# Folding the score maxima by DMA before they are turned, and turning the rows of both norms beside them

## The chip, the cores and the metric

The kernel runs on one core of a Trainium2 chip. A core has five engines that each take their own instructions in the written order and wait for one another by semaphores: PE (TensorE, matrix products and turns, written to PSUM), DVE (VectorE), ACT (ScalarE), POOL (GpSimd) and SP (SyncE, which here only issues DMAs). The metric is the device time of one execution in microseconds (us), the median over runs of the same kernel. A lower time is better.

## The reference, cut to what matters

One adaptive-norm transformer block on 8 sequences of 1024 tokens with 256 features: a norm with modulation, attention with 16 heads of 64 over 1024 keys, a gated residual, a second norm, and a mixture of 8 experts in which each expert takes its 512 best tokens. All of it is float32.

```python
h = _layernorm(x) * (1 + ca) + sa
q, k, v = ...                                  # einsum('bpv,havn->bhapn', h, w_qkv)
scores = einsum('bhqn,bhkn->bhqk', q, k) / sqrt(64)
attn = softmax(scores, axis=-1)                # exp(scores - max over keys), by its sum
x = x + ga * (einsum('bhqk,bhkn->bhqn', attn, v) ... @ w_o)
h = _layernorm(x) * (1 + cb) + sb
x = x + gb * ffn(h)                            # router, top 512 tokens of each of 8 experts, two layers
```

The change lies in the maximum over keys of the softmax and in the turning of the rows of both norms.

## The kernel before

The attention stage is a software pipeline. A **unit** `u` is one pair of heads of one sequence and half of its queries (512): 8 sequences x 8 pairs x 2 halves are 128 units (`NSU`). The 1024 keys of a unit are 8 blocks of 128 (`c`), and a **group** `g` is two of those blocks, so that a unit has four groups; `gm` is the group within the unit. The loop at L648 goes through the groups and writes each engine's instructions in the order in which the engine takes them: everything stands in a manual schedule.

For a block of keys, `scores_mm` (L306) makes two products, one for each head `j`, with keys on the partitions and queries along the free dimension, in one of two PSUM buffers with the tag "s". `scores_out` (L319) copies them to SBUF on ScalarE (L322) and folds them into a running maximum `top` of 128 x (2 x 512) on VectorE (L327). After the last block, `top` holds for every query 128 candidates, one per partition.

`max_turn` (L329) turns `top` on PE against an identity as eight blocks of 128 x 128 into a third use of the "s" buffers, so that the candidates of a query lie along the free dimension; `split_max` (L338) reduces them on VectorE over 128 x 1024 elements to 128 x 8 negated maxima and splits each into three bfloat16 parts (L342 to L350). `max_rows` (L352) turns the parts back to rows on PE, ScalarE copies the rows (L361), and `max_spread` (L363) adds the three parts by a product with ones, so that `less` has the negated maximum in every partition. `subtract` (L371), `exp_of` (L374), `values_mm` (L377) and POOL's `add_up` (L395) follow with a delay: subtractions of unit `u` start five groups after its first scores, values six.

In a group the order is: steps booked under "load" (DMAs), the spread, one or two delayed subtractions, the scores of two blocks with copies and maxima, the steps "m1" (projections `qk_task` and `v_task`, one in each group but the first; `max_rows` in the first), "post", the exponentials, two value products, in the last group `max_turn` and `split_max`, then "pool" and "m2". The work of other stages is booked into groups by `at(g, where, f, ...)`. Two of those stages turn rows of a norm: `ln_out` (L243, first norm, 32 calls) and `out_turn` (L522, second norm, 32 calls of which 28 lie in the pipeline). Both make a turn of 128 x 128 as two matmuls of 64 columns against the identity. `free_slot` (L597) gives these steps, and the output projection `out_proj` (L488), one slot each in a last group of a unit, behind the turn of the maxima. The denominators go through DRAM: `den_out`, `den_load`, `den_inv`, `den_spread`, `den_mul` (L408 to L469).

All DMAs of this stage are issued from SyncE, in the order of the program. After the pipeline come the tail of the last sequence, the search for each expert's tokens and the experts.

Of the kernel before, what the change touches and what calls it, by code (L numbers as in the profile page):

```python
# [28 lines left out]
F32 = mybir.dt.float32  # L29
BF16 = mybir.dt.bfloat16  # L30
# [12 lines left out]
def adaln_block(  # L43
# [171 lines left out]
    def at(g, where, f, *args):  # L215
        steps.setdefault((g, where), []).append((f, args))
# [26 lines left out]
    def ln_out(b, t):  # L243
        if t == 0:
            hTs[b] = work.tile([P, KC, S], F32, tag="hT", name=f"hT{b}")
        xt = ln_x.pop((b, t))[0]
        pt = ps_m.tile([P, KC, 2 * P], F32, tag="mm", name=f"ptx{b}_{t}")
        for k in range(KC):
            for i in range(2):
                for m in range(2):  # L250
                    c0 = k * P + m * N
                    nc.tensor.matmul(
                        pt[m * N : (m + 1) * N, k, i * P : (i + 1) * P],
                        xt[:, i, c0 : c0 + N], ident, start=True, stop=True,
                    )
        for k in range(KC):
            nc.vector.tensor_scalar(
                hTs[b][:, k, 2 * t * P : (2 * t + 2) * P], pt[:, k, :],
                modT[:, KC + k, b : b + 1], modT[:, k, b : b + 1],
                op0=ALU.mult, op1=ALU.add,  # L260
            )

    def ln_task(b, t, g):
        at(g - 4, "load", ln_load, b, t)
        at(g - 2, "post", ln_stats, b, t)
        at(g - 1, "pool", ln_norm, b, t)
        at(g, "m2", ln_out, b, t)


    def qk_task(b, p, i):  # L270
# [48 lines left out]
    def scores_out(u, c, ps):  # L319
# [6 lines left out]
            tops[u] = work.tile([P, 2, QB], F32, tag="top", name=f"top{u}", bufs=1)  # L326
        nc.vector.tensor_tensor(tops[u], probs[u, 0] if c == 1 else tops[u], ps, ALU.max)  # L327

    def max_turn(u):  # L329
        top = tops.pop(u)  # L330
        turned[u] = ps_s.tile([P, 8, P], F32, tag="s", name=f"tt{u}")
        for j in range(2):
            for t in range(4):
                nc.tensor.transpose(  # L334
                    turned[u][:, 4 * j + t, :], top[:, j, t * P : (t + 1) * P], ident
                )

    def split_max(u):  # L338

        tt = turned.pop(u)  # L340
        nm = tt[:, :2, :8]
        nc.vector.tensor_reduce(nm[:, 0, :], tt, AX.X, ALU.max, negate=True)  # L342
        part = [
            parts_of[u % 2][:, :, :, i].rearrange("p t j -> p j t") for i in range(3)
        ]
        whole, rest = (nm[:, i, :].rearrange("p (j t) -> p j t", j=2) for i in range(2))
        nc.vector.tensor_copy(part[0], whole)
        nc.vector.tensor_sub(rest, whole, part[0])
        nc.vector.tensor_copy(part[1], rest)
        nc.vector.tensor_sub(part[2], rest, part[1])  # L350

    def max_rows(u):  # L352
        pn = ps_m.tile([P, QB], BF16, tag="mm", name=f"pn{u}")
        for t in range(4):
            for j in range(2):
                nc.tensor.transpose(
                    pn[j * N : (j + 1) * N, t * P : (t + 1) * P],
                    parts_of[u % 2][:, t, j, :], ident_b,
                )
        rows_of[u] = work.tile([P, QB], BF16, tag="nr", name=f"nr{u}")  # L360
        nc.scalar.copy(rows_of[u], pn)  # L361

    def max_spread(u):  # L363

        less[u] = ps_b.tile([P, 2, QB], F32, tag="less", name=f"less{u}")
        rows = rows_of.pop(u)
        for j in range(2):
            r = slice(j * N, (j + 1) * N)
            nc.tensor.matmul(less[u][:, j, :], three[r, :], rows[r, :], start=True, stop=True)  # L369

    def subtract(u, c):  # L371
        nc.vector.tensor_tensor(probs[u, c], probs[u, c], less[u], ALU.add)  # L372
# [127 lines left out]
    def out_add(b, t, po):  # L500
        n = f"{b}_{t}"
        x1 = o_x[b, t]
        tmp = small.tile([P, D], F32, tag="at", name=f"at{n}", bufs=2)
        nc.vector.tensor_mul(tmp, po, mods[b][:, 0, :])
        nc.vector.tensor_add(x1[:, 0, :], x1[:, 0, :], tmp)
        nc.sync.dma_start(out[b, t * P : (t + 1) * P, :], x1[:, 0, :])
        o_h[b, t] = stats_of(small, x1, 1, f"b{n}")

    def out_norm(b, t):
        n = f"{b}_{t}"  # L510
        mv = o_h[b, t]
        rs = rstd_of(small, mv, 1, f"b{n}")
        x1 = o_x.pop((b, t))[:, 0, :]
        row = small.tile([P, ROW], F32, tag="row", name=f"row{n}", bufs=6)
        h2 = row[:, :D]
        eng = nc.vector if b == B - 1 else nc.gpsimd
        eng.tensor_scalar(h2, x1, mv[:, 0, 0:1], rs, op0=ALU.subtract, op1=ALU.mult)
        nc.gpsimd.tensor_mul(h2, h2, mods[b][:, 2, :])
        nc.gpsimd.tensor_add(h2, h2, mods[b][:, 1, :])
        o_h[b, t] = row  # L520

    def out_turn(pool, b, t, tag="mm"):  # L522

        n = f"{b}_{t}"
        pt = pool.tile([P, 2, KC, P], F32, tag=tag, name=f"pth{n}")
        for i in range(2):
            h2 = o_h[b, t + i]
            for k in range(KC):
                for m in range(2):
                    c0 = k * P + m * N  # L530
                    nc.tensor.matmul(
                        pt[m * N : (m + 1) * N, i, k, :], h2[:, c0 : c0 + N], ident,
                        start=True, stop=True,
                    )
        h2T = small.tile([P, 2, KC, P], F32, tag="h2T", name=f"h2T{n}", bufs=1)
        nc.scalar.copy(h2T, pt)
        o_x[b, t] = h2T
# [54 lines left out]
        )  # L592


    taken = set()

    def free_slot(g, behind=False):  # L597
        while g in taken or g % 4 == 0 or behind != (g % 4 == 3):
            g += 1
        taken.add(g)  # L600
        return g

    for t in range(NT // 2):
        ln_task(0, t, -23 + 3 * t)
        ln_task(1, t, free_slot(39 + 4 * t, True))
    for b in range(B):
        for p in range(NP):
            P0 = 8 * (b * NP + p)
            for i, g in enumerate((-7, -6, -5, -2)):
                at(P0 + g, "m1", qk_task, b, p, i)  # L610
            if p % 2 == 0:
                for t, g in enumerate((-9, -3, -1, 5)):
                    at(P0 + g, "m1", v_task, b, p // 2, t)
            if (b, p) == (B - 1, NP - 1):
                continue

            at(P0 + 17, "load", den_load, b, p)
            at(P0 + 18, "post", den_inv, b, p)
            at(P0 + 19, "load", den_spread, b, p)
            at(P0 + 20, "pool", den_mul, b, p)  # L620
        if b + 1 < B:
            if b + 2 < B:
                for t in range(NT // 2):
                    ln_task(b + 2, t, free_slot(64 * (b + 1) + 39 + 4 * t, True))
            for t in range(NT):
                g = free_slot(64 * (b + 1) + 19 + 4 * t, True)
                at(g - 2, "load", out_load, b, t)
                at(g, "m2", out_proj, ps_m, b, t)
                at(g + 1, "pool", out_norm, b, t)
                if t % 2:  # L630
                    g = free_slot(g + 2, True)
                    at(g, "m2", out_turn, ps_m, b, t - 1)
                    g = free_slot(g + 1)
                    at(g, "m2", out_route, ps_m, b, t - 1)
                    at(g + 1, "post", out_exp, b, t - 1)
                    at(g + 2, "post", out_score, b, t - 1)
                    at(g + 3, "pool", out_store, b, t - 1)
    for u in range(NSU):
        at(4 * u + 4, "m1", max_rows, u)
        if u < NSU - 1:  # L640
            at(4 * u + 12, "m2", den_out, u)
    for b in range(B):
        at(64 * b + 30, "load", gates, b)
    for t in range(NT):
# [2 lines left out]
    with tc.manual_schedule():  # L647
        g = -28  # L648
        while g < 4 * NSU + LAG or steps:
            u, gm = divmod(g, 4)  # L650
            run(g, "load")
            if gm == 1 and 0 < u <= NSU:
                max_spread(u - 1)
            u1, gm1 = divmod(g - LAG + 1, 4)
            late = [(u1, 2 * gm1 + i) for i in range(2) if 0 <= u1 < NSU]

            for uc in late[: 1 if gm == 3 else 2]:
                subtract(*uc)
            if 0 <= u < NSU:
                for c in (2 * gm, 2 * gm + 1):  # L660
                    scores_out(u, c, scores_mm(u, c))
            if gm == 3 and late:
                subtract(*late[1])
            run(g, "m1")
            run(g, "post")
            for uc in late:
                exp_of(*uc)
            u1, gm1 = divmod(g - LAG, 4)
            if 0 <= u1 < NSU:
# [7 lines left out]
                    values_out(u1)  # L677
                if u1 < NSU - 1:
                    add_up(u1, gm1)
            if gm == 3 and 0 <= u < NSU:  # L680
                max_turn(u)
                split_max(u)
            run(g, "pool")
            run(g, "m2")
            g += 1
# [342 lines left out]
```

## Time and profile before

| | us |
|---|---|
| median of 3 runs | 3648.16 (3646.65 to 3648.54) |
| profiled execution, its own time | 3645.84 |
| its span, first to last instruction | 3644.1 |
| PE busy | 3467.5 (95%) |
| DVE busy | 2902.9 (80%) |
| ACT busy | 2431.7 (67%) |
| POOL busy | 2668.6 (73%) |
| turn of the maxima, L334 on PE | 139.9 in 1024 instructions |
| reduction of the turned maxima, L342 on DVE | 157.4 in 128 |
| turns of the norms, L252 and L531 on PE | 39.0 and 39.6 in 512 instructions each |
| eviction of the first norm's turn, L257 on DVE | 31.7 in 64 |

Busy time is a union of the intervals in which an engine works; matmuls of one kind overlap, so that busy time over the count is less than the mean duration. A line such as `L334 PE MATMUL tt<-ident,top` names the line of the kernel, the engine, the operation, the tile written and those read. In a timeline the first column is the start in us from the span's start, the second the time that the merged instructions take; in brackets stands how long the engine was idle before them and who released it. In a list of waits, the numbers are the total in us, the count and the longest. DMA-issuing instructions on SyncE are short and don't contain the transfer.

### The profile page before, as it was taken

What the parts mean: (1) busy time and instruction counts of PE and PEld (TensorE: products, weight loads), DVE (VectorE), ACT (ScalarE), POOL (GpSimd) and SP (SyncE); (2) the same over time, 40 slices, a digit from 0 to 9 for tenths busy, and PEclk for the clock granted to TensorE, in tenths of its full rate; (3) what the DMA queues carried; (4) which work ended last, traced back from release to release, by engine and by line L of the source; (5) the groups of instructions that cost most, each with busy time, mean ns of one, the idle gap of its engine ahead of it and who ended that gap; (6) DMA issues with size and microseconds to landing.
All of it is one profiled execution on the core that took longest, in us unless ns stands there. A gap on an engine that the chain in (4) does not pass through costs nothing. (4 is left out here: it accounts for less than half of the span.)

```text
span 3644.1 us, 54310 instructions
## 1 busy us (share of the span) xinstructions
PE 3467.5 (95%) x20670; PEld 1461.3 (40%) x20670; DVE 2902.9 (80%) x3647; ACT 2431.7 (67%) x2978; POOL 2668.6 (73%) x1545
## 2 busy tenths in 40 slices
PE   5999999999999999999999999999999999982898
PEld 2333334334343444344343343344434334442565
DVE  3888888888888888888888888888888888857442
ACT  1777777777777777777777777777777777740111
POOL 1678777887788778888788888887888787851232
PEclk8999999999999999999999999999999999995999
DMA  3010002111120112011210113111211112133332
GB/s 76 7 39 27 24 31 58 49 38 45 45 62 30 52 48 66 29 45 45 62 52 29 51 50 62 30 50 46 62 38 43 46 48 59 51 85 122 93 99 41
DMA packets 189045, 185.40 MB, mean 51 GB/s; under 512 B 48856, under 2 KB 167144, under 8 KB 188656
## 3 DMA queue, kind: packets, MB, share of 16 engines
q1 hardware_dynamic: 159856, 156.62, 15.1%
q0 software_dynamic: 7168, 12.72, 1.7%
q10 hardware_dynamic: 21760, 12.59, 1.3%
q8 instruction: 163, 2.67, 0.3%
q14 instruction: 98, 0.80, 0.1%
HBM read 127.06 MB, written 63.21 MB: 52 GB/s over the span
## 5 line engine op out<-in xcount | busy, mean ns | idle before, releaser
L403 POOL TENSOR_TENSOR acc<-acc,p 128x1024 f32<-128x1024 f32 x762 | 1806.5, 2371 | 360.0 <-ACT p L375 327.0
L322 ACT COPY p<-s 128x1024 f32<-128x1024 f32 x1024 | 996.4, 1018 | 421.7 <-PE s L313 415.0
L372 DVE TENSOR_TENSOR p<-p,less 128x1024 f32<-128x1024 f32 x1024 | 1206.5, 1209 | 32.6 <-PE less L369 30.0
L327 DVE TENSOR_TENSOR top<-top,s 128x1024 f32<-128x1024 f32 x768 | 936.6, 1220 | 260.3 <-ACT p L322 219.3
L375 ACT ACTIVATE p<-p 128x1024 f32<-128x1024 f32 x1024 | 1041.8, 1057 | 74.7 <-DVE p L372 74.4
L313 PE MATMUL s<-qk,qk 64*128 64x512 f32 x4096 | 1025.8, 613 | 35.2 <-DVE parts L350 32.1
L384 PE MATMUL av<-p,v 128*64 128x512 f32 x4096 | 967.1, 593 | 1.8 <-ACT oT L393 1.8
L313 PEld LDWEIGHTS s<-qk,qk 64*128 64x128 f32 x4096 | 358.9, 187 | 527.4 <-issue 237.8
L278 PE MATMUL pq<-hT,wq 128*64 128x512 f32 x2048 | 495.9, 605 | 2.7 <-ACT qk L285 1.4
L384 PEld LDWEIGHTS av<-p,v 128*64 128x64 f32 x4096 | 280.6, 137 | 461.4 <-issue 366.9
L400 POOL TENSOR_TENSOR acc<-p,p 128x1024 f32<-128x1024 f32 x127 | 301.6, 2375 | 176.2 <-ACT p L375 176.2
L278 PEld LDWEIGHTS pq<-hT,wq 128*64 128x64 f32 x2048 | 124.2, 136 | 342.7 <-issue 211.4
L295 PE MATMUL pv<-wq,hT 128*64 128x256 f32 x2048 | 250.7, 387 | 2.6 <-ACT qk L283 1.4
L953 ACT ACTIVATE h<-ph,b_sb 128x512 f32<-128x512 f32 x64 | 44.0, 687 | 276.1 <-PE ph L949 276.1
L342 DVE TENSOR_REDUCE tt<-tt 128x8 f32<-128x1024 f32 x128 | 157.4, 1229 | 67.6 <-PE tt L334 67.5
L494 PE MATMUL po<-wo,ot 128*64 128x256 f32 x1792 | 205.7, 382 | 0.0
L295 PEld LDWEIGHTS pv<-wq,hT 128*64 128x64 f32 x2048 | 136.5, 137 | 155.7 <-issue 66.5
L327 DVE TENSOR_TENSOR top<-p,s 128x1024 f32<-128x1024 f32 x128 | 155.7, 1217 | 32.3 <-ACT p L322 32.3
L300 ACT COPY v<-pv 128x512 f32<-128x512 f32 x128 | 75.0, 586 | 148.4 <-PE pv L295 148.4
L334 PEld LDWEIGHTS tt<-ident,top 128*128 128x128 f32 x1024 | 109.6, 140 | 107.2 <-DVE top L327 107.2
L465 POOL TENSOR_TENSOR oT<-oT,rb 128x1024 f32<-128x1024 f32 x63 | 150.0, 2381 | 3.0 <-issue 3.0
L494 PEld LDWEIGHTS po<-wo,ot 128*64 128x64 f32 x1792 | 123.5, 137 | 66.2 <-issue 9.4
(161 smaller groups left out, 2442.8 us busy)
## 6 DMA issues: line engine op xcount, KB each, us to landing
rb<-rden_d SPq DMA_DIRECT2D x128, 256.0 KB
oT_d<-oT SPq DMA_DIRECT2D x62, 512.0 KB
ot<-oT_d SPq DMA_DIRECT2D x56, 512.0 KB
rows_d<-row SPq DMA_DIRECT2D x64, 132.0 KB
lnx<-in_L_attn_inputs_dram SPq DMA_DIRECT2D x32, 256.0 KB
rows_d<-gb_d SPq DMA_DIRECT2D x8, 1024.0 KB
w<-in_L_ffn_w_dram ACTq DMA_DIRECT2D x8, 1024.0 KB
w<-in_L_ffn_w_dram SPq DMA_DIRECT2D x8, 1024.0 KB
```

What stands on the lines that cost most here:

```text
L278: nc.tensor.matmul(pq[m * N : (m + 1) * N, :], wq[:, k, a, 2 * p + m, :], hTs[b][:, k, sl], start=(k == 0), stop=(k == KC - 1),)
L295: nc.tensor.matmul(pv[m * N : (m + 1) * N, i, :], hTs[b][:, k, t0 : t0 + N], wq[:, k, 2, 4 * g : 4 * g + 4, :], start=(k == 0), stop=(k == ...
L313: nc.tensor.matmul(ps[:, j, :], kt[r, c * P : (c + 1) * P], qt[r, h * QB : (h + 1) * QB], start=True, stop=True,)
L322: nc.scalar.copy(probs[u, c], ps)
L327: nc.vector.tensor_tensor(tops[u], probs[u, 0] if c == 1 else tops[u], ps, ALU.max)
L342: nc.vector.tensor_reduce(nm[:, 0, :], tt, AX.X, ALU.max, negate=True)
L372: nc.vector.tensor_tensor(probs[u, c], probs[u, c], less[u], ALU.add)
L375: nc.scalar.activation(probs[u, c], probs[u, c], AF.Exp)
L384: nc.tensor.matmul(avs[u][j * N : (j + 1) * N, :], v[:, c, hh * N : (hh + 1) * N], pT[:, j, :], start=(c == 0), stop=(c == NT - 1),)
L400: nc.gpsimd.tensor_tensor(sums[u], pts[0], pts[1], ALU.add)
L403: nc.gpsimd.tensor_tensor(sums[u], sums[u], pt, ALU.add)
L494: nc.tensor.matmul(po[m * N : (m + 1) * N, :], ot[:, p, m * N : (m + 1) * N], wo[:, p, :], start=(p == 0), stop=(p == NP - 1),)
```

## The change

`max_fold` is new: after the last maximum of a unit, four DMAs from SyncE copy the 64-partition halves of `top` into two tiles of 128 x 512 floats, so that partitions 0 to 63 hold head 0 and partitions 64 to 127 hold head 1, each with half of the candidates. `max_halves` takes the larger of the two on VectorE, in the first group of the next unit, between its two subtractions. `max_turn` then has four blocks instead of eight, written to PSUM behind that group's two scores, and `split_max` reduces 128 x 512 elements. Both stand in the first group of the next unit, behind "m1". A new kind of step, "turn", follows them at once, and the rows of both norms are turned there by four transposes of 128 x 128 for a call instead of eight matmuls of 64 columns. The first norm's eviction goes to ScalarE. `max_rows` moves from "m1" to "m2" of that group, the spread moves behind the scores of the second group, and the split of the subtractions ahead of and behind the scores changes with it. The first norm of the next sequence is booked earlier, the output projection goes to the third group of a unit, the denominator's steps move by one group, and three tiles (`nr`, `at`, `row`) get fewer buffers.

```diff
@@ -247,24 +247,20 @@
         pt = ps_m.tile([P, KC, 2 * P], F32, tag="mm", name=f"ptx{b}_{t}")
         for k in range(KC):
             for i in range(2):
-                for m in range(2):
-                    c0 = k * P + m * N
-                    nc.tensor.matmul(
-                        pt[m * N : (m + 1) * N, k, i * P : (i + 1) * P],
-                        xt[:, i, c0 : c0 + N], ident, start=True, stop=True,
-                    )
+                nc.tensor.transpose(
+                    pt[:, k, i * P : (i + 1) * P], xt[:, i, k * P : (k + 1) * P], ident
+                )
         for k in range(KC):
-            nc.vector.tensor_scalar(
-                hTs[b][:, k, 2 * t * P : (2 * t + 2) * P], pt[:, k, :],
-                modT[:, KC + k, b : b + 1], modT[:, k, b : b + 1],
-                op0=ALU.mult, op1=ALU.add,
+            nc.scalar.activation(
+                hTs[b][:, k, 2 * t * P : (2 * t + 2) * P], pt[:, k, :], AF.Identity,
+                bias=modT[:, k, b : b + 1], scale=modT[:, KC + k, b : b + 1],
             )
 
     def ln_task(b, t, g):
         at(g - 4, "load", ln_load, b, t)
         at(g - 2, "post", ln_stats, b, t)
         at(g - 1, "pool", ln_norm, b, t)
-        at(g, "m2", ln_out, b, t)
+        at(g, "turn", ln_out, b, t)
 
 
     def qk_task(b, p, i):
@@ -326,24 +322,38 @@
             tops[u] = work.tile([P, 2, QB], F32, tag="top", name=f"top{u}", bufs=1)
         nc.vector.tensor_tensor(tops[u], probs[u, 0] if c == 1 else tops[u], ps, ALU.max)
 
+    def max_fold(u):
+
+        top = tops[u]
+        tops[u] = [work.tile([P, QB], F32, tag=f"half{i}", name=f"half{i}_{u}", bufs=1) for i in range(2)]
+        for i in range(2):
+            for j in range(2):
+                src = (i + j) % 2
+                nc.sync.dma_start(
+                    tops[u][i][j * N : (j + 1) * N, :], top[src * N : (src + 1) * N, j, :]
+                )
+
+    def max_halves(u):
+        a, b = tops[u]
+        nc.vector.tensor_tensor(a, a, b, ALU.max)
+
     def max_turn(u):
-        top = tops.pop(u)
-        turned[u] = ps_s.tile([P, 8, P], F32, tag="s", name=f"tt{u}")
-        for j in range(2):
-            for t in range(4):
-                nc.tensor.transpose(
-                    turned[u][:, 4 * j + t, :], top[:, j, t * P : (t + 1) * P], ident
-                )
+        top = tops.pop(u)[0]
+        turned[u] = ps_s.tile([P, 2, QB], F32, tag="s", name=f"tt{u}")
+        for t in range(4):
+            sl = slice(t * P, (t + 1) * P)
+            nc.tensor.transpose(turned[u][:, 0, sl], top[:, sl], ident)
 
     def split_max(u):
 
         tt = turned.pop(u)
-        nm = tt[:, :2, :8]
-        nc.vector.tensor_reduce(nm[:, 0, :], tt, AX.X, ALU.max, negate=True)
-        part = [
-            parts_of[u % 2][:, :, :, i].rearrange("p t j -> p j t") for i in range(3)
-        ]
-        whole, rest = (nm[:, i, :].rearrange("p (j t) -> p j t", j=2) for i in range(2))
+        nm = tt[:, 1, :16].rearrange("p (i t j) -> p i t j", i=2, j=2)
+        part = [parts_of[u % 2][:, :, :, i] for i in range(3)]
+        whole, rest = nm[:, 0], nm[:, 1]
+        nc.vector.tensor_reduce(
+            whole, tt[:, 0, :].rearrange("p (t j k) -> p t j k", t=4, j=2), AX.X, ALU.max,
+            negate=True,
+        )
         nc.vector.tensor_copy(part[0], whole)
         nc.vector.tensor_sub(rest, whole, part[0])
         nc.vector.tensor_copy(part[1], rest)
@@ -357,7 +367,7 @@
                     pn[j * N : (j + 1) * N, t * P : (t + 1) * P],
                     parts_of[u % 2][:, t, j, :], ident_b,
                 )
-        rows_of[u] = work.tile([P, QB], BF16, tag="nr", name=f"nr{u}")
+        rows_of[u] = work.tile([P, QB], BF16, tag="nr", name=f"nr{u}", bufs=1)
         nc.scalar.copy(rows_of[u], pn)
 
     def max_spread(u):
@@ -500,7 +510,7 @@
     def out_add(b, t, po):
         n = f"{b}_{t}"
         x1 = o_x[b, t]
-        tmp = small.tile([P, D], F32, tag="at", name=f"at{n}", bufs=2)
+        tmp = small.tile([P, D], F32, tag="at", name=f"at{n}", bufs=1)
         nc.vector.tensor_mul(tmp, po, mods[b][:, 0, :])
         nc.vector.tensor_add(x1[:, 0, :], x1[:, 0, :], tmp)
         nc.sync.dma_start(out[b, t * P : (t + 1) * P, :], x1[:, 0, :])
@@ -511,7 +521,7 @@
         mv = o_h[b, t]
         rs = rstd_of(small, mv, 1, f"b{n}")
         x1 = o_x.pop((b, t))[:, 0, :]
-        row = small.tile([P, ROW], F32, tag="row", name=f"row{n}", bufs=6)
+        row = small.tile([P, ROW], F32, tag="row", name=f"row{n}", bufs=4)
         h2 = row[:, :D]
         eng = nc.vector if b == B - 1 else nc.gpsimd
         eng.tensor_scalar(h2, x1, mv[:, 0, 0:1], rs, op0=ALU.subtract, op1=ALU.mult)
@@ -526,12 +536,7 @@
         for i in range(2):
             h2 = o_h[b, t + i]
             for k in range(KC):
-                for m in range(2):
-                    c0 = k * P + m * N
-                    nc.tensor.matmul(
-                        pt[m * N : (m + 1) * N, i, k, :], h2[:, c0 : c0 + N], ident,
-                        start=True, stop=True,
-                    )
+                nc.tensor.transpose(pt[:, i, k, :], h2[:, k * P : (k + 1) * P], ident)
         h2T = small.tile([P, 2, KC, P], F32, tag="h2T", name=f"h2T{n}", bufs=1)
         nc.scalar.copy(h2T, pt)
         o_x[b, t] = h2T
@@ -592,17 +597,9 @@
         )
 
 
-    taken = set()
-
-    def free_slot(g, behind=False):
-        while g in taken or g % 4 == 0 or behind != (g % 4 == 3):
-            g += 1
-        taken.add(g)
-        return g
 
     for t in range(NT // 2):
         ln_task(0, t, -23 + 3 * t)
-        ln_task(1, t, free_slot(39 + 4 * t, True))
     for b in range(B):
         for p in range(NP):
             P0 = 8 * (b * NP + p)
@@ -614,31 +611,28 @@
             if (b, p) == (B - 1, NP - 1):
                 continue
 
-            at(P0 + 17, "load", den_load, b, p)
-            at(P0 + 18, "post", den_inv, b, p)
-            at(P0 + 19, "load", den_spread, b, p)
-            at(P0 + 20, "pool", den_mul, b, p)
+            at(P0 + 18, "load", den_load, b, p)
+            at(P0 + 19, "post", den_inv, b, p)
+            at(P0 + 20, "load", den_spread, b, p)
+            at(P0 + 21, "pool", den_mul, b, p)
         if b + 1 < B:
-            if b + 2 < B:
-                for t in range(NT // 2):
-                    ln_task(b + 2, t, free_slot(64 * (b + 1) + 39 + 4 * t, True))
+            for t in range(NT // 2):
+                ln_task(b + 1, t, 64 * b + 4 + 4 * t)
             for t in range(NT):
-                g = free_slot(64 * (b + 1) + 19 + 4 * t, True)
+                g = 64 * (b + 1) + 18 + 4 * t
                 at(g - 2, "load", out_load, b, t)
                 at(g, "m2", out_proj, ps_m, b, t)
                 at(g + 1, "pool", out_norm, b, t)
                 if t % 2:
-                    g = free_slot(g + 2, True)
-                    at(g, "m2", out_turn, ps_m, b, t - 1)
-                    g = free_slot(g + 1)
-                    at(g, "m2", out_route, ps_m, b, t - 1)
-                    at(g + 1, "post", out_exp, b, t - 1)
-                    at(g + 2, "post", out_score, b, t - 1)
-                    at(g + 3, "pool", out_store, b, t - 1)
+                    at(g + 6, "turn", out_turn, ps_m, b, t - 1)
+                    at(g + 9, "m2", out_route, ps_m, b, t - 1)
+                    at(g + 10, "post", out_exp, b, t - 1)
+                    at(g + 11, "post", out_score, b, t - 1)
+                    at(g + 12, "pool", out_store, b, t - 1)
     for u in range(NSU):
-        at(4 * u + 4, "m1", max_rows, u)
+        at(4 * u + 4, "m2", max_rows, u)
         if u < NSU - 1:
-            at(4 * u + 12, "m2", den_out, u)
+            at(4 * u + 13, "m2", den_out, u)
     for b in range(B):
         at(64 * b + 30, "load", gates, b)
     for t in range(NT):
@@ -649,19 +643,30 @@
         while g < 4 * NSU + LAG or steps:
             u, gm = divmod(g, 4)
             run(g, "load")
-            if gm == 1 and 0 < u <= NSU:
-                max_spread(u - 1)
             u1, gm1 = divmod(g - LAG + 1, 4)
             late = [(u1, 2 * gm1 + i) for i in range(2) if 0 <= u1 < NSU]
 
-            for uc in late[: 1 if gm == 3 else 2]:
+            early = {0: 2, 1: 0, 2: 2, 3: 1}[gm]
+            for i, uc in enumerate(late[:early]):
                 subtract(*uc)
+                if gm == 0 and i == 0 and 0 < u <= NSU:
+                    max_halves(u - 1)
             if 0 <= u < NSU:
                 for c in (2 * gm, 2 * gm + 1):
                     scores_out(u, c, scores_mm(u, c))
-            if gm == 3 and late:
-                subtract(*late[1])
+                if gm == 3:
+                    max_fold(u)
+            if gm == 1 and 0 < u <= NSU:
+                max_spread(u - 1)
+            for uc in late[early:]:
+                subtract(*uc)
             run(g, "m1")
+            if gm == 0 and 0 < u <= NSU:
+                if not late:
+                    max_halves(u - 1)
+                max_turn(u - 1)
+                split_max(u - 1)
+            run(g, "turn")
             run(g, "post")
             for uc in late:
                 exp_of(*uc)
@@ -677,9 +682,6 @@
                     values_out(u1)
                 if u1 < NSU - 1:
                     add_up(u1, gm1)
-            if gm == 3 and 0 <= u < NSU:
-                max_turn(u)
-                split_max(u)
             run(g, "pool")
             run(g, "m2")
             g += 1
```

## The prediction

> **What bounds the kernel now.** I read the stretches first. Three windows cut the attention stage into its start, a part and the rest; the columns are the stretch, then PE, PEld, DVE, ACT and POOL busy with instruction counts, granted clock, DMA share and GB/s.
>
> ```profile
> 85.00:600.00 515.00, 492.71 (x2740) 185.45 (x2740) 431.16 (x474) 393.10 (x471) 389.91 (x183) 1.00 0.10 28
> 600.00:1112.00 512.00, 509.57 (x3086) 204.40 (x3084) 437.70 (x530) 382.58 (x467) 420.94 (x239) 1.00 0.18 49
> 1112.00:3219.00 2107.00, 2094.05 (x12680) 840.21 (x12677) 1803.15 (x2153) 1577.29 (x1927) 1720.05 (x973) 1.00 0.17 47
> ```
>
> From 600 us on PE is busy 99.5% of the time at full clock; DVE is at 86%, ACT at 75%, POOL at 82%. The 128 units of the attention stage fill 85 to 3219 us, 24.7 us each, and PE sets that. So PE work removed is time won, and **any new wait on PE is time lost**, as PE takes its work in the written order.
>
> Next the waits, all engines, for what PE itself still waits on near the change:
>
> ```profile
> DVE top L327 <- ACT p L322: 251.6, 243, 22.4
> DVE tt L342 <- PE tt L334: 67.5, 99, 1.2
> PE s L313 <- DVE parts L350: 32.1, 71, 1.3
> ```
>
> PE loses 32.1 us to the split maxima (71 waits, because the turned maxima hold a scores buffer). Then the order of time, around the end of one unit:
>
> ```profile
> 1499.44 1.99 PE L313 MATMUL s<-qk,qk 64*128 64x512 f32 x8
> ...
> 1501.36 1.94 PE L278 MATMUL pq<-hT,wq 128*64 128x512 f32 x8
> 1501.72 2.55 DVE L327 TENSOR_TENSOR top<-top,s 128x1024 f32<-128x1024 f32 x2 [1.07 <-ACT p L322]
> 1503.13 1.89 PE L384 MATMUL av<-p,v 128*64 128x512 f32 x8
> ...
> 1504.18 1.21 DVE L372 TENSOR_TENSOR p<-p,less 128x1024 f32<-128x1024 f32 x1
> 1504.94 1.09 PE L334 MATMUL tt<-ident,top 128*128 128x128 f32 x8
> ...
> 1505.97 1.09 PE L252 MATMUL ptx<-ident,lnx 128*64 128x128 f32 x16
> 1506.08 1.23 DVE L342 TENSOR_REDUCE tt<-tt 128x8 f32<-128x1024 f32 x1 [0.68 <-PE tt L334]
> ...
> 1508.00 0.19 DVE L350 TENSOR_TENSOR parts<-tt,parts 128x8 bf16<-128x8 f32 x1
> ...
> 1509.40 0.41 PE L356 MATMUL pn<-ident_b,parts 128*64 128x128 bf16 x8
> ```
>
> Call the end of the unit's last scores (1501.43) zero. The last maximum ends at 2.84 in nearly every unit. PE reaches the turn at 3.51, only 0.67 later: the chain is covered by one projection and one value block. In this order PE is hardly ever early.
>
> Last, how long a transfer of this kind takes until an engine can use it. The nearest is the reciprocal spread, two DMAs of 256 KB, each to 64 partitions (512 KB, as much as one fold). The SyncE timeline and the VectorE timeline, in the tail where nothing hides it:
>
> ```profile
> 3251.47 1.68 SPq L456 DMA_DIRECT2D rb<-rden_d  x2
> 3256.35 1.23 DVE L463 TENSOR_TENSOR oT<-oT,rb 128x1024 f32<-128x1024 f32 x1 [6.95 <-DMA rb<-rden_d]
> ```
>
> 4.88 us from issue to use, and the stretch of one such pair in the middle, by its packets:
>
> ```profile
> 1549.75:1552.20 2.45, 2.45 (x14) 0.69 (x10) 2.35 (x3) 1.71 (x3) 2.37 (x2) 1.00 0.87 212
> ```
>
> [...] here packets begin 0.8 to 1.3 us after the issue begins, and the consumer starts 0.4 to 0.8 us after the last packet. [...] the trace's one such row (L856) has 693. [...]
>
> **The change, part by part.** Costs are per unit, 127 units; start-to-start times in the trace are used where PE blocks follow each other (turn of eight blocks 1.02, norm turn 1.02, scores 1.81 to 1.92, values 1.82).
>
> 1. Maxima turned as four blocks: 8 x 0.128 becomes 4 x 0.128. Minus 0.51.
> 2. Norm turns. L252 and L531 have 512 records each for 32 calls: 16 per call in 1.02 us, two records per float32 matmul. Four transposes at the 0.128 of L334 are 0.51. Minus 0.51 in 64 calls, 0.26 per unit.
> 3. The scores' wait for the parts goes, since the turn now comes behind the first two scores and the third finds a free buffer: minus 32.1/127 = 0.25.
> Sum of gains: 1.02 per unit, **130 us**.
> 4. Added on VectorE: one maximum over 512 columns, 0.69; the reduction falls from 1.23 to about 0.70 (512 columns less at 1.04 ns, as between its row and the small ones). The four splitting steps stay, 0.88 with gaps. The norm's eviction (64 x 0.535) leaves VectorE for ScalarE, some 0.4 each by the 256-column copy of L427 (0.377); ScalarE has 25% free. Shifts of the denominator steps by one group, and moved norm loads: nothing, covered by a group of 5.5 us or more; without it POOL's multiply and the store would be late by one transfer. Fewer buffers (row 4, at 1, nr 1): nothing by the written order, as row t-1 is stored in the group ahead of row t+3's norm; if the store is late, POOL waits.
> 5. Added on SyncE: four DMAs of 128 KB per unit, 64 packets of 2 KB for each. Ahead of them in SyncE's queue are the stores that wait for POOL's product and VectorE's x1; both are due a group earlier. Behind them stand the reciprocal's store, the next loads and the spread, which are needed a group or more later.
> 6. **The new waits.** VectorE: the halves' maximum stands between the two subtractions of the next unit's first group, and the second subtraction, the next maximum, the reduction and the splits are queued behind it. PE: the turn stands right behind the first two scores, with norm turn and values behind it; then max_rows, which has moved behind the values, waits for the parts. The turn also takes the buffer of the next unit's first scores, free when ScalarE has copied them, near 6.2 by its order (exp after the 4.05 of the subtraction, then the copy); the halves come later than that in every case below but the second rival.
>
> Let X be the time from the last maximum's end to the fold's use. Issues back to back are 0.43 to 0.58 apart, so the fourth starts at 1.6 and could land at 1.6 + 0.8 + 0.4 + 0.4 = 3.2, if each only adds its own tail. [...] X = 1.0 to first packets + 2.45 + 0.6 = 4.1. Upper end: the spread's 4.88 in the tail. A bound below all: VectorE has two subtractions ahead, 2 x 1.22 = 2.45. I take **X = 4.1** as the bytes and half-width match.
>
> The walk from zero: last maximum 2.84. It is 0.75 later in the 56 units whose out projection moves to the group before: its product, sum and statistics (0.42 + 0.43 + 0.43 + 0.18, with gaps 1.76) and a subtraction (1.22) precede the last two maxima; on average 0.33. Then X; halves 0.74; subtraction 1.23; maximum 1.24; reduction 0.73; splits 0.85; and 0.15 for semaphores. That is 8.11 + X until max_rows can start. PE's own work up to there: 3.52 + scores 1.85 + turn 0.51 + norm turn 0.24 (60 of 128 units) + values 1.82 + route 0.11 (28 units) = 8.05. So PE stands still for X + 0.06, **4.16 us per unit**, first at the turn, then at max_rows. Nothing gives it back: after max_rows PE again sets the pace and VectorE, near 22 us of work in 28, waits for scores.
>
> Sum: 127 x (4.16 - 1.02) = +399 us on the profiled 3645.84 (span 3644.1 and 1.7 around it), 4045; the median of the runs is 2.3 above that, so **4047**. I say 4040, the splits' semaphores being rounded up.
>
> **The rivals.**
> - *The fold is quick.* X falls to the 2.45 of the two subtractions: stall 2.51, +189, 3837. For it: [...] the tail's spread had other loads beside it. Against: issue alone takes 1.6 us and the first packets 0.8.
> - *PE work decides, faster.* If VectorE and ScalarE run far enough ahead that halves and parts are ready when PE asks, only the 130 us of gains remain: 3518. It needs X at most 1.6 for the turn (3.52 + 1.85 = 5.37 less 2.84, the halves' 0.74 and a semaphore), and the parts by 8.05. Against it: the last maximum hangs on the last scores at a constant 2.84, so nothing can run ahead. For it: 86% VectorE, 99.5% PE.
> - *Only the first stall costs*, the parts being ready behind the values: the stall is 2.84 + 0.33 + 4.1 + 0.84 - 5.37 = 2.74, +218, 3866.
> - *The fold queues* behind rb, ot or the 1 MB gates, or waits in SyncE's order for a store: X = 6, stall 6.06, +640, 4288. Against: in the written order those loads come behind the fold, and DMA share is 0.17.
> - *No difference*: stall equal to gains, X near -1 on the path; only if several steps fail.
>
> **How the numbers follow.** Chances: fold as costed (X 3.2 to 4.9: 3930 to 4150) 0.62; quick fold or first stall alone 0.20; queueing 0.09; faster 0.08; same 0.01. The likeliest gives 4040. The range runs from the quick fold, 3830, to X = 4.9, 4150, and leaves out the faster case and queueing. Within 0.2% (7 us) is about what a measurement of this kernel can tell from no change. Slower: 0.91.
>
> **What would show it.** Right: a VectorE wait of the halves' maximum on a fold DMA, some 1 to 2 us in each unit; PE waits of the turn on that maximum and of max_rows on the parts, together about 500 us; PE's busy share in the middle near 85%; turns of 0.5 us. A last-maximum-to-use time of 3.2 or less makes my X wrong; PE at 99% makes the walk wrong; parts ready ahead of max_rows make the second stall wrong.

## The result, and the profile after

The changed kernel takes **4411.41 us** (4410.58 to 4416.24), against 3648.35 for the kernel before on the same chip: ratio 1.2096, 95% interval 1.2079 to 1.2113. The prediction said slower, 4040, at most 4150. The profiled execution took 4416.24 with a span of 4414.3.

Busy times of the page after; its first line, then two of its groups:

```profile
PE 3641.8 (83%) x19390; PEld 1505.6 (34%) x19390; DVE 2995.4 (68%) x3711; ACT 2488.0 (56%) x3042; POOL 2685.9 (61%) x1545
...
L345 PE MATMUL tt<-ident,half 128*128 128x128 f32 x512 | 127.2, 397 | 530.8 <-DVE half L338 530.8
...
L338 DVE TENSOR_TENSOR half<-half,half 128x512 f32<-128x512 f32 x128 | 202.8, 1585 | 285.7 <-DMA half<-top 285.7
```

PE has fewer instructions than before (20670) and yet is busy 174 us longer: part of its work runs slower. The turn waited 530.8 us for the halves, the halves 285.7 us for the fold. And the halves' maximum (L338) takes 1585 ns in the mean, where the prediction counted 0.74 us with its gap, from a row of 693 ns (L856 of the kernel before, 128x512).

PE's waits after, in total, count and longest, in the list of PE's waits:

```profile
PE tt L345 <- DVE half L338: 530.8, 128, 10.6
PE pq L274 <- ACT den L437: 86.2, 123, 1.0
```

The end of a unit in order of time:

```profile
1896.86 1.99 PE L309 MATMUL s<-qk,qk 64*128 64x512 f32 x8
...
1899.59 2.35 POOL L413 TENSOR_TENSOR acc<-acc,p 128x1024 f32<-128x1024 f32 x1
...
1901.12 1.37 DVE L338 TENSOR_TENSOR half<-half,half 128x512 f32<-128x512 f32 x1 [1.69 <-DMA half<-top]
...
1902.59 1.09 PE L345 MATMUL tt<-ident,half 128*128 128x128 f32 x4 [3.74 <-DVE half L338]
...
1903.61 3.68 PE L394 MATMUL av<-p,v 128*64 128x512 f32 x8
...
1906.06 0.20 DVE L360 TENSOR_TENSOR parts<-tt,parts 128x8 bf16<-128x8 f32 x1
1907.07 0.64 PE L366 MATMUL pn<-ident_b,parts 128*64 128x128 bf16 x8
```

The halves' maximum begins while POOL's running sum is under way and ends at 1902.49, 0.55 us after that sum. The value products behind the turn take 3.68 us instead of 1.89, the four turned blocks 1.09, what eight took before. Three stretches around it, with the granted clock third from the end, show why:

```profile
1894.00:1902.50 8.50, 4.85 (x40) 2.17 (x36) 6.67 (x9) 5.83 (x9) 7.71 (x7) 0.92 0.28 64
1902.50:1909.00 6.50, 6.41 (x26) 2.86 (x28) 3.62 (x7) 1.64 (x2) 4.60 (x2) 0.58 0.00 0
1909.00:1922.00 13.00, 12.30 (x62) 3.75 (x58) 11.05 (x13) 10.09 (x13) 4.19 (x4) 1.00 0.07 22
```

Around the gap of 3.74 us PE's granted clock falls to 0.58 in the mean of a stretch, and it is full again in the next one. The clock's mean over the run is 0.911, before 0.979. max_rows, at 1907.07, no longer waits for the parts, which are there at 1906.26; the slow values are later.

The unit in the trace, mean over 96 units, from the end of its last scores, in us (the fold time X runs from the last maximum's end to the start of the halves' maximum; the predicted unit is the 24.82 of before plus the net 3.14 of the prediction):

| | before | predicted | after |
|---|---|---|---|
| last maximum ends | 2.85 | 3.17 | 3.41 |
| X | | 4.1 | 4.60 (median 4.31) |
| halves' maximum | | 0.74 | 1.60 |
| parts ready | 7.09 | 12.1 | 13.38 |
| max_rows starts | 8.98 | 12.2 | 14.18 |
| one unit | 24.82 | 27.96 | 30.96 |

### The profile page after: what moved, and what is told of

The parts are those of the page before. It is cut to its first block, busy times and chain, and to the rows that moved or that the text cites. A ratio compares the mean times of both kernels' runs of the same rounds, so it can differ in the third digit from the quotient of the medians.

```text
span 4414.3 us, 52937 instructions
## 1 busy us (share of the span) xinstructions
PE 3641.8 (83%) x19390; PEld 1505.6 (34%) x19390; DVE 2995.4 (68%) x3711; ACT 2488.0 (56%) x3042; POOL 2685.9 (61%) x1545
## 5 line engine op out<-in xcount | busy, mean ns | idle before, releaser
L385 ACT ACTIVATE p<-p 128x1024 f32<-128x1024 f32 x1024 | 1061.5, 1055 | 484.5 <-DVE p L382 474.9
L394 PE MATMUL av<-p,v 128*64 128x512 f32 x4096 | 1146.1, 687 | 5.9 <-ACT oT L403 5.9
L274 PE MATMUL pq<-hT,wq 128*64 128x512 f32 x2048 | 499.4, 608 | 88.9 <-ACT den L437 86.2
L345 PE MATMUL tt<-ident,half 128*128 128x128 f32 x512 | 127.2, 397 | 530.8 <-DVE half L338 530.8
L394 PEld LDWEIGHTS av<-p,v 128*64 128x64 f32 x4096 | 314.0, 155 | 581.3 <-issue 535.7
L338 DVE TENSOR_TENSOR half<-half,half 128x512 f32<-128x512 f32 x128 | 202.8, 1585 | 285.7 <-DMA half<-top 285.7
L345 PEld LDWEIGHTS tt<-ident,half 128*128 128x128 f32 x512 | 83.1, 199 | 633.0 <-issue 461.7
L371 ACT COPY nr<-pn 128x512 bf16<-128x512 bf16 x128 | 74.8, 584 | 226.3 <-PE pn L366 226.3
L514 DVE TENSOR_TENSOR at<-po,mod 128x256 f32<-128x256 f32 x56 | 23.8, 425 | 207.1 <-PE po L504 207.1
```

The lines of the kernel that those rows point to most:

```text
L274: nc.tensor.matmul(pq[m * N : (m + 1) * N, :], wq[:, k, a, 2 * p + m, :], hTs[b][:, k, sl], start=(k == 0), stop=(k == KC - 1),)
L345: nc.tensor.transpose(turned[u][:, 0, sl], top[:, sl], ident)
L385: nc.scalar.activation(probs[u, c], probs[u, c], AF.Exp)
L394: nc.tensor.matmul(avs[u][j * N : (j + 1) * N, :], v[:, c, hh * N : (hh + 1) * N], pT[:, j, :], start=(c == 0), stop=(c == NT - 1),)
```

## The experiments

All ratios are to the kernel before, with 95% intervals. My theory after the result (A): the fold's latency stalls PE as predicted, and three things come on top: the halves' maximum stands behind POOL, the gap halves PE's clock, and the projection waits for the denominator's copy. The main rival (B): the new order itself costs, with a fold or without.

**e1, one part alone.** In both norm turns of the kernel before:

```diff
-                for m in range(2):
-                    c0 = k * P + m * N
-                    nc.tensor.matmul(
-                        pt[m * N : (m + 1) * N, i, k, :], h2[:, c0 : c0 + N], ident,
-                        start=True, stop=True,
-                    )
+                nc.tensor.transpose(pt[:, i, k, :], h2[:, k * P : (k + 1) * P], ident)
```

> The kernel before with one part of the change: the rows of both norms are turned by four transposes a call instead of eight matmuls of 64 columns. If the term of the sum was right (64 calls, 1.02 us down to 0.51 us each, all on PE's path), 33 us less: 3616 us. If mixing 128-column blocks into the 64-column work costs PE something, or the turns are hidden, 3640 us or more.

3643.56 us, 0.9990 (0.9983 to 0.9997): 3 us less, where 33 were forecast. The list of PE's waits says where they went:

```profile
PE s L310 <- DVE parts L347: 64.6, 71, 1.3
```

The turns did become 0.5 us shorter, and the wait for the parts behind them grew from 32.1 to 64.6 us. So in the units whose norm is turned there, the kernel before seems to be bound by the chain from the turn to the next scores, and PE's work there only fills it (e7, e8 and e11 test this). The "99.5% busy" did not show that.

**e2, no fold, the turn where it was.** From the changed kernel, fold and halves go, and the turn of eight blocks returns to the end of the unit:

```diff
-                if gm == 3:
-                    max_fold(u)
...
+            if gm == 3 and 0 <= u < NSU:
+                max_turn(u)
+                split_max(u)
             run(g, "pool")
```

> The changed kernel with fold and halves taken out and the turn of eight blocks put back at the end of the unit's last group, all other moves kept (norm turns, max_rows behind the values, out projection in the third group, denominators one group later). Theory A (the loss sits in the fold and in what its gap does to PE): the norm turns win 33 us and PE's new wait of the projection on the denominator's copy, 0.68 us in 127 units, costs 86: about 3700 us, clock 0.98. Theory B (the new order costs, fold or no fold): 3900 us or more.

3927.06 us, 1.0763 (1.0745 to 1.0781). Theory A's 3700 was wrong by far: the order without a fold costs 280 us. PE waits 123.5 us for the parts (99 times), 115.5 for the denominator's copy, 28.5 for the last maximum.

**e3, no fold, the turn where the change has it.** As e2, but `max_turn` and `split_max` stay in the next unit's first group, with two buffers for `top`.

> The changed kernel with fold and halves taken out, the turn of eight blocks standing where the change has it, behind the next unit's first two scores (two buffers for the running maximum). By the prediction's walk without a transfer: the turn at 6.2 us after the last scores, parts at 10.6, PE waiting 2.1 us a unit: with the denominator's wait about 3925 us, waits under 2 us each and a clock near 0.98. Theory B: over 4200 us. Theory that the fold is all of the loss: under 3750 us.

3961.61 us, 1.0864 (1.0846 to 1.0882), clock 0.979. Waits as the walk had them: 135.2 us of max_rows for the parts, 122.3 of the turn for ScalarE's copy of the next scores. So of the 763 us, some 315 are the order without the four-block turn's gain, and the fold with all that hangs on it adds 450. A and B each hold in part.

**e9, the projection alone.** In the kernel before:

```diff
-                g = free_slot(64 * (b + 1) + 19 + 4 * t, True)
+                g = 64 * (b + 1) + 18 + 4 * t
```

> The kernel before with only the output projection booked in the third group of a unit, as the change has it, instead of behind the turn in the last group. If the projection was what covered the way from the turn to the parts, 56 more units wait for the parts, about 1.2 us each, and the last maxima come later behind its sums: about 3750 us. If it is PE work wherever it stands, 3647 us.

3842.80 us, 1.0537 (1.0519 to 1.0554), twice the loss expected. The parts are waited for 121 times instead of 71 (137.7 us), the turn waits 53.2 us for a last maximum that now ends 0.8 us later on average, and the clock falls to 0.972. One cause of the late maximum is in VectorE's list, the projection's second addition in the kernel before and here:

```profile
L505 DVE TENSOR_TENSOR ox<-ox,at 128x256 f32<-128x256 f32 x56 | 23.9, 426 | 1.9
L505 DVE TENSOR_TENSOR ox<-ox,at 128x256 f32<-128x256 f32 x56 | 88.8, 1586 | 1.9
```

At its new place it began in all 56 cases while a POOL sum ran. The other part, the projection's 3.6 us behind the turn having covered the chain, is read from the waits.

**e10, denominators back.** As e2, with `at(4 * u + 12, "m2", den_out, u)` in place of `4 * u + 13`.

> As e2, with the denominators' product back in the first group of a unit, ahead of max_rows. If the projection's wait for the denominator's copy (115.5 us on PE in e2) is a cost of its own, about 3830 us. If that wait only takes the place of another, about 3927 us as e2.

4002.45 us, 1.0974 (1.0956 to 1.0993), slower than e2 by 75. The projection's wait is gone, but max_rows, now behind the denominators' product in the same single PSUM buffer, waits 129.7 us for the same copy, and the turn waits 70.2 us for the last maximum instead of 28.5. What that wait costs by itself is not settled by this.

**e4, PE kept busy.** The changed kernel with work for the gap:

```diff
+                fill = ps_m.tile([P, QB], F32, tag="mm", name=f"fill{u}")
+                for _ in range(4):
+                    nc.tensor.matmul(
+                        fill, ident, hTs[min(u, NSU - 1) // 16][:, 0, :QB], start=True, stop=True
+                    )
                 max_turn(u - 1)
```

> The changed kernel with four more float32 products of 128x128 by 512 columns (0.94 us each, 3.8 us in all) on PE in front of the turn, where it waits for the halves; nobody uses their result. Theory A, in which the idle gap halves PE's clock for what follows it: the clock returns to 0.98, the values behind the turn to 1.8 us, and the time falls although PE has 480 us more of work, to about 4280 us. If only the waiting counts and the clock doesn't: 4411 us or more.

4308.51 us, 1.1810 (1.1790 to 1.1829): **103 us less with 470 us more of PE work**, and a clock of 0.982. The timeline of the same unit:

```profile
1902.12 3.70 PE L669 MATMUL fill<-hT,ident 128*128 128x512 f32 x8
1905.65 0.60 PE L345 MATMUL tt<-ident,half 128*128 128x128 f32 x4
1906.18 1.94 PE L394 MATMUL av<-p,v 128*64 128x512 f32 x8
1909.03 0.41 PE L366 MATMUL pn<-ident_b,parts 128*64 128x128 bf16 x8 [0.91 <-DVE parts L360]
```

Turn and values have their full speed again, and max_rows waits for the parts, as the prediction had it.

**e5, half the fold.** `for i in range(1)` in `max_fold`, and the halves' maximum takes its one tile twice.

> The changed kernel with two of the four fold DMAs: the second tile isn't filled and the halves' maximum takes the first one twice, so that half of the candidates are left out of the maximum. Same places and instructions otherwise. If the fold's time is issue and half-width transfer, the time from the last maximum to the halves falls from 4.3 to about 2.9 us, the gap on PE falls under 3 us, the clock returns to 0.98, and the run takes about 4120 us. If a fixed completion time is nearly all of it, 3.9 us or more and 4350 us.

4186.12 us, 1.1473 (1.1457 to 1.1490). X is 3.00 in the median against 4.31: two DMAs of 128 KB are 1.3 us, so most of X is not a fixed time. Whether issue or transfer scales isn't settled, as both went. The time fell less than expected and the clock came back only to 0.942: the halves' maximum now takes either 0.69 or up to 2.7, and where it is long the gap on PE is still near 4 us.

**e6, a quiet POOL.** In `add_up`, the additions behind the first pair of key blocks are left out, so that the denominators are incomplete.

> The changed kernel without POOL's running sums beyond the first pair of key blocks, so that the softmax's denominators are left incomplete and POOL is nearly idle. If the halves' maximum is slow because it stands behind a POOL instruction that reads SBUF, it takes 0.69 us in every unit instead of 1.6, and the run about 4270 us. If it is slow by itself or the landing isn't over when it begins, it stays at 1.6 and the run at 4411.

4202.87 us, 1.1530 (1.1514 to 1.1547). The halves' maximum, from the view of the tile:

```profile
L338 DVE TENSOR_TENSOR half<-half,half x128: 684/692/694, 92.9 to 3772.7; 128x512 f32<-128x512 f32 x128
```

In the changed kernel the same row is:

```profile
L338 DVE TENSOR_TENSOR half<-half,half x128: 686/1529/2384, 96.3 to 3987.6; 128x512 f32<-128x512 f32 x128
```

There it began 119 times while a POOL sum ran, and ended 0.55 us after that sum's end (0.545 to 0.554); nine times POOL was idle, and it took 0.69. So here it waits for the running POOL sum. The subtractions and the running maxima, whose second operand lies in PSUM, keep their 1.21 and 1.22 us in the changed kernel; 374 and 468 of them began during a POOL instruction of over 2 us, and none of these took more than 1.22.

The run fell by 209 us, 67 more than expected. POOL had held up a second instruction that the expectation did not see, the moved projection's second addition. In the changed kernel and here it is:

```profile
L515 DVE TENSOR_TENSOR ox<-ox,at 128x256 f32<-128x256 f32 x56 | 63.6, 1136 | 1.9
L514 DVE TENSOR_TENSOR ox<-ox,at 128x256 f32<-128x256 f32 x56 | 23.8, 424 | 1.9
```

In the changed kernel all 56 began while a POOL sum ran and ended 0.28 us after it. Without that the last maximum ends at 3.06 instead of 3.41, and the clock is 0.931 instead of 0.911.

**e12, both.** e6 with three filling products.

> The changed kernel with both: POOL's sums left out as in e6 (denominators incomplete) and three filling products in front of the turn (2.8 us, as the gap is 3.0 there). If the clock is a cost of its own beside POOL's, max_rows starts right behind the parts, near 12.2 us after the last scores, the clock is 0.98, and the run takes about 4145 us against e6's 4203. If the clock's loss is hidden once the halves are quick, 4203 us.

4155.56 us, 1.1397 (1.1378 to 1.1416), clock 0.979, max_rows at 12.21 behind parts at 12.14. The clock is a cost of its own beside POOL's, but only 47 us of e4's 103 are left for it when POOL is quiet. With both undone the run stands 116 us over the prediction.

**e7, the parts later.** e1 with the reduction cut in two, one for each head.

> The kernel before with the norm turns as single transposes (as in e1) and the reduction of the turned maxima cut in two, one for each head, so that the first can start after four blocks. Theory: at the end of a unit the kernel before is bound by the chain turn, reduction, splits, next scores, and the norm turns only filled that wait. Then parts come 0.4 us earlier in the 71 units that wait: about 3615 us. If PE's work bounds it, the time of e1, 3643 us.

3657.47 us, 1.0032 (1.0020 to 1.0044), slower than e1 by 14. The first reduction didn't start before the eighth block; the cut only made the parts 0.20 us later. PE's wait for the parts grew by the same 14 us, from 64.6 to 78.6: the miss shows from the other side that the parts set the time there.

**e8, the turn ahead of the values.** e1, and in `scores_out` and the loop:

```diff
+        if c >= 6:
+            nc.vector.tensor_tensor(tops[u], tops[u], ps, ALU.max)
+            nc.scalar.copy(probs[u, c], ps)
+            return
         nc.scalar.copy(probs[u, c], ps)
...
             run(g, "m1")
+            if gm == 3 and 0 <= u < NSU:
+                max_turn(u)
+                split_max(u)
             run(g, "post")
```

> As e1, with the maxima of the last two key blocks taken ahead of ScalarE's copies of them, and the turn of eight blocks ahead of the value products of that group instead of behind them: no DMA, same work. If the chain to the parts bounds the end of a unit, PE's wait for the parts (64.6 us in e1) goes and the run takes about 3580 us. If something else is next, such as ScalarE's later copies, 3640 us.

**3592.44 us, 0.9852 (0.9839 to 0.9865), faster than both kernels.** The last maximum ends at 1.74 instead of 2.84, the parts are ready at 5.18 instead of 7.09, and PE waits for them no longer; what is left on PE in this stretch is

```profile
PE tt L335 <- DVE top L320: 7.9, 5, 2.7
```

**e11, the same without the norm turns of e1.**

> As e8, but with the norms turned in eight matmuls of 64 columns as in the kernel before. With the chain ahead of PE, the norm turns should be worth the 33 us of the prediction's sum, which they were not in e1: e8 plus 33, about 3625 us. If they are worth nothing there either, 3592 us.

3612.20 us, 0.9901 (0.9885 to 0.9918). With the chain out of the way the norm turns are worth about 20 us, not 3 and not 33; where the other 13 go stays open.

## Why the prediction was right and wrong

**Right:** the sign, the place and the way. PE stood still at the turn for the fold, and nothing later gave it back. The walk without a transfer (e3) came out at 3962 where it gave 3925, but with the denominator's wait added, which the prediction did not have. The fold was near in size, 4.31 in most units for 4.1; that it is paced as the spread is, by its width of 64 partitions, was an estimate and is not shown. In the kernel before the spread's stretch moved 212 GB/s, and the 1.4 us from 1513.80, with the 128-partition store in them, 360 GB/s. But in the fold's packets the four issues lie 0.53 to 0.65 apart, packets begin 1.14 after the first issue and last 2.69, and VectorE starts 0.45 after them; the pace of the issues fits that as well. The moved eviction loaded no table: the kernel after has one table load as before. The faster rival was far off.

**Luck:** PE's stall, forecast at 4.16 us per unit, is 530.8 us or 4.18. But the forecast put 2.74 at the turn and the rest at max_rows. All of the measured stall is at the turn, 1.4 us longer there than forecast; behind it PE did not wait for the parts, it ran slowly.

**Wrong:** the size, 399 us for 763. The sum counted waits alone and priced each instruction as if it ran undisturbed. The steps that failed, as the prediction put them:

- "halves 0.74" in the walk: 1.60 on average. The price came from a row that ran with POOL idle. 0.86 in 127 units are 109 us.
- The moved projection's sum of 0.43, in the walk's 0.33 for a later last maximum: the sum took 1.14 behind POOL, and the delay is 0.57. With a quiet POOL it is 0.21 (e6). In the old order the same move costs 194 us (e9).
- "Nothing gives it back": true of the wait, but the sum had no term for the clock. The list of stretches before showed full clock, where PE had no such gap. Filling the gap won 103 us (e4). In the changed kernel the granted clock is 0.50 from 1901.2 to 1908.0, around the gap shown above, and 1.00 from 1908.1 to 1931.8. In its attention stage, 123 of 127 gaps on PE of 3.0 us or more were followed by 2 us with a mean clock under 0.75, and none of 123 gaps under 1.1 us. In e6, where the turn's gaps are 3.0 in the mean (331.7 us in 110), 88 of 106 of 2.2 to 3.0 us brought half clock too, and none of 71 between 0.7 and 1.6. The prediction had a stall of 4.16 us and did not ask.
- "I take X = 4.1", and in the queueing rival "those loads come behind the fold": the 1 MB gates are booked one group ahead of it. In the 8 units where they are (unit 7 of each sequence), and in no others, X is 7.9 to 12.5 us. These are some 40 us, and 0.23 in the other units 27.
- "after max_rows PE again sets the pace": the projection waits for the denominator's copy, 86.2 us. Part 4 called the shifted denominators free by the time of a group; it looked at the transfers and not at the single PSUM buffer in front of the next projection.
- Gain 2, norm turns, 33 us on PE's path: 3 us in e1. The path at that place was the chain to the parts.

By the runs, the 371 us between the forecast 4040 and the measured 4411 divide so: 209 go when POOL is quiet (e6), 47 more when the gap is filled as well (e12), and 116 stay. Of the 209, my estimate from the unit times is 116 for the halves' maximum and 44 for the last maximum; the rest goes with the better clock. The 116 that stay are of the size of the gates and the denominator's wait, but no run takes either out alone (e10 only moves the second), so that part is read from waits and stays open. The list of what would show it held in PE's busy share in the middle (84%) but for a mixed reason, since slow work counts as busy, and failed in the turns of 0.5 us (1.09 in most) and in the wait of max_rows for the parts. The wait of the halves for the fold, 285.7 us or 2.25 a unit, is a little over its 1 to 2.

## What to carry to other kernels

Price a new wait on PE together with what the gap does to the products behind it (here the values took 3.68 us instead of 1.89), and a VectorE instruction on two SBUF tiles together with what POOL is doing at that moment (here 1.60 us on average instead of 0.69). A PE that is 99.5% busy can still be bound by a chain at one place, and work that stands there may be cover and not cost: before moving it, ask what waits behind it. Here a turn that hung on a late maximum was helped by making both earlier (e8), not by making the turn smaller.

## What was not expected of the hardware

The halves' maximum ended a constant 0.55 us after the running POOL instruction whatever its own start, so its cost is the rest of a 2.39 us POOL instruction and 0.55 us; for the smaller addition (L515) the constant is 0.28. And idle PE was dearer than useless work: 470 us of products that nobody reads made the run 103 us shorter.
